# Attention scores from split halves of q and k in float32r, and maxima with a separate mask pass

## The chip, the cores and the metric

The kernel runs on one core of a Trainium2 chip. The metric is the device time of one execution in microseconds. A core has five engines that run their own instruction streams: TensorE (PE; its weight loads are shown apart as PEld), VectorE (DVE), ScalarE (ACT), GpSimd (POOL) and SyncE (SP), which here only issues DMAs. Engines wait for one another through semaphores. SBUF is the working memory of 128 partitions; TensorE writes to PSUM, which has eight banks of 128 partitions by 512 float32 numbers.

## The reference, cut to what matters

One transformer block for 8 batches of 1024 tokens of width 256, with 16 heads of 16 dimensions each. `ca`, `sa`, `ga`, `cb`, `sb` and `gb` are rows computed from a small conditioning input.

```python
h = _layernorm(x, axis=-1) * (1 + ca) + sa
qkv = jnp.einsum('bnd,ed->bne', h, w_in)
...
scores = jnp.einsum('bhqd,bhkd->bhqk', q, k) * Hd ** (-0.5)
scores = jnp.where(causal, -jnp.inf, scores)
attn = jax.nn.softmax(scores, axis=-1)
out = jnp.einsum('bhqk,bhkd->bhqd', attn, v)
...
x = x + ga * (out @ w_out.T + b_out)
h = _layernorm(x, axis=-1) * (1 + cb) + sb
xr = mu_r * h + (1.0 - mu_r) * h_prev      # h_prev: h one token earlier
xk = mu_k * h + (1.0 - mu_k) * h_prev
x = x + gb * (sigmoid(xr @ W_r.T) * (square(relu(xk @ W_k.T)) @ W_v.T))
```

The change concerns the causal scores, their maxima over the keys, and the exponentials of score minus maximum.

## The kernel before, in words

**Units, steps and strips.** Attention is worked in units of four heads: `u` counts 32 units, four to a batch. Four heads lie on the 128 partitions in strips of 32 (`ST`): 16 partitions with the head's q or k, the rest padding. A matmul over one strip uses 32 rows of TensorE, so four heads can run beside one another. A unit has nine steps (`STEPS`, `ORDER`): a to e are the blocks on the causal diagonal, 0 to 3 the whole blocks below it. Each step covers about 512 score columns for each of the four heads. A pass over a unit is made twice.

- In the pass **S** (`maxima`, line 513) the queries stand on the partitions of the result: tile `pp` (two heads of one half, two PSUM banks, from a pool of two such tiles). VectorE takes maxima over the keys. On the diagonal this is one custom instruction per head and part, which adds the mask and reduces, with an accumulator read behind it (`largest`, 548); below the diagonal one reduction over two heads.
- `subtract` (577) turns the maxima of 512 queries by a TensorE transpose (`pmx`), negates them on ScalarE (`mrow`) and sends them by one DMA into a padding row of the unit's q tile, where k has ones. So the maximum is subtracted by the product itself.
- In the pass **T** (`weights`, 604) the keys stand on the partitions of the result: tiles `pw`, one bank each from a pool of four that nearly all other products share. ScalarE takes the exponentials, GpSimd zeroes the blocks' upper triangle. `attend` (652) multiplies with v into `po`, some steps at a time (`GROUPS`).

The pass T follows S by `LAG` = 9 steps (line 54), that is by one unit. `step` (1060) records one step: the DMAs that have come due (`transfers`, 155; urgent ones first), the products of both passes, the reductions and exponentials, and then a list of other work placed by hand in the tables `POST`, `PREP` and `END` (1150 to 1186): the projections and layer norms of the next batch, the feed-forward part of the batch before. S takes its steps in the order a, 0, b, e, c, d, 1, 2, 3, T in the order of `ORDER`.

**Order on the engines.** The wrapper `InOrder` (115) keeps each engine's instructions in the order in which they are recorded. All of them therefore have line 125 in the profile, and the reader goes by tile names. All DMAs but three go through SP's queue, where a transfer that waits holds all that follow.

**q and k.** `qk` (448) projects 128 columns of q or k for 512 tokens, ScalarE scales or copies them (`qk`, three buffers), and one DMA writes them into padded scratch in DRAM. `to_chip` (502) loads q and k of a unit back, in strips, into one of `KEPT` = 4 pairs of tiles, by two DMAs. For units 0 and 1 `direct` (489) computes them in place from weights that are padded already.

**Scores.** In `maxima` and `weights` each block is one float32 matmul per head:

```python
pe.matmul(
    pw[n2][:, cols],
    kk[rs, kt * P : (kt + 1) * P],
    q[rs, c * CW + lo : (c + 1) * CW],
    start=True,
    stop=True,
)
```

With both passes under way, first the products of T for heads 0 and 1 are issued beside those of S for heads 2 and 3, then the other way round, part by part.

Of the kernel before, what the change touches and what calls it, by code (L numbers as in the profile page):

```python
# [8 lines left out]
F32 = mybir.dt.float32  # L9
AF = mybir.ActivationFunctionType  # L10
# [19 lines left out]
KEPT = 4  # L30
# [42 lines left out]
def adaln_block(  # L73
# [94 lines left out]
    def load_xa(b, c):  # L168

        place = dict(tag="xb", bufs=3) if (b, c) == (0, 1) else dict(tag="xa")  # L170
        A[b, c]["xa"] = sb.tile([P, NT, D], F32, name=f"xa{b}_{c}", **place)
        sync.dma_start(A[b, c]["xa"], tokens(x, b, c))
# [40 lines left out]
    wgate = const.tile([P, DC, 2, D], F32, tag="wgate", name="wgate")  # L213
# [22 lines left out]
    q_of, k_of = [], []  # L236
    for u in range(KEPT):
        q_of.append(const.tile([P, N], F32, tag=f"q{u}", name=f"q{u}"))
        k_of.append(const.tile([P, N], F32, tag=f"k{u}", name=f"k{u}"))

    zero = const.tile([P, 1], F32, tag="zero", name="zero")
    one = const.tile([P, 1], F32, tag="one", name="one")
    pool.memset(zero, 0.0)
    pool.memset(one, 1.0)

    def clear_strips(u):
        act.copy(q_of[u], zero.to_broadcast([P, N]))
        act.copy(k_of[u], one.to_broadcast([P, N]))
# [4 lines left out]
    for n in range(2 * NC):  # L253
# [3 lines left out]
    padded_of = [  # L257
        [
            [
                dram.tile([NC, 2 * HG, ST, CW], F32, tag=f"pad{m}{n}{half}", name=f"pad{m}{n}{half}")  # L260
                for half in range(2)
            ]
            for n in range(2)
        ]
        for m in range(2)
    ]

    def clear_dram(m, half):
        for n, of in enumerate((q_of[3], k_of[3])):
            for c in range(NC):  # L270
                sync.dma_start(padded_of[m][n][half][c, :, HD:, :], of[:, :CW])
# [7 lines left out]

    def row_of(t):  # L280

        return strips(t)[:, HD, :]
# [57 lines left out]
    def fold(b, n):  # L340
        gate = G[b]["gates"]
        name, of = (("wo", wo_sb), ("wv", wfv_sb))[n]
        G[b][name] = sb.tile([P, DC, D], F32, tag=f"{name}b", bufs=2, name=f"{name}b{b}")
        for c in range(DC):
            pool.tensor_mul(G[b][name][:, c, :], of[:, c, :], gate[:, n * D : (n + 1) * D])
        if n == 0:
            G[b]["bias"] = sb.tile([P, D], F32, tag="biasb", bufs=2, name=f"biasb{b}")
            pool.tensor_mul(G[b]["bias"], b_bc, gate[:, :D])
# [79 lines left out]
    def prep(b, c):  # L428
# [19 lines left out]
        def qk(n, half):  # L448
# [7 lines left out]
            w = sb.tile([P, CW], F32, tag="qk", bufs=3, name=f"qk{b}_{c}_{n}_{half}")  # L456
            if n == 0:
                act.mul(w, pq, SCALE)
            else:
                act.copy(w, pq)  # L460

            later(lambda: sync.dma_start(padded_of[b % 2][n][half][c, :, :HD, :], w))
# [25 lines left out]

    def direct(c, n, g):

        pq = bank(f"pd{c}_{n}_{g}")
        for d in range(DC):
            of = padded[d][:, n * H + g * HG : n * H + (g + 1) * HG, :].rearrange("p h e -> p (h e)")
            by_strips(pq, of, A[0, c]["hT"][:, d, :], d == 0, d == DC - 1)
        to = (q_of, k_of)[n][g][:, c * CW : (c + 1) * CW]
        if n == 0:
            act.mul(to, pq, SCALE)
        else:

            act.activation(to, pq, AF.Identity, bias=below)  # L500

    def to_chip(u):

        b, g = divmod(u, NG)
        for n, of in enumerate((q_of, k_of)):
            heads = slice(g % 2 * HG, (g % 2 + 1) * HG)
            sync.dma_start(
                of[u % KEPT].rearrange("p (c n) -> p c n", c=NC),
                padded_of[b % 2][n][g // 2][:, heads].rearrange("c h s n -> (h s) c n"),
            )  # L510


    def maxima(u, k, half):
# [3 lines left out]
        q, kk = q_of[u % KEPT], k_of[u % KEPT]  # L517
        js = (2 * half, 2 * half + 1)
        pp = ps_s.tile([P, 2, CW], F32, tag="s", name=f"pp{u}_{k}_{half}")
        parts, at = [], 0  # L520
        for c, i, diagonal in STEPS[k]:
            if ("max", c) not in V:

                V["max", c] = sb.tile(
                    [P, c + 1, HG * NT], F32, tag=f"max{c}", bufs=2, name=f"max{u}_{c}"
                )
            t = NT - 1 - i if diagonal else i
            n = (t + 1) * P if diagonal else CW
            parts.append((c, t, slice(at, at + n), diagonal))
            at += n  # L530

        def products(m):
            if m >= len(parts):
                return
            c, t, cols, diagonal = parts[m]
            q0 = c * CW + t * P
            k0 = c * CW if diagonal else 0
            for n2, j in enumerate(js):
                rs = slice(j * ST, (j + 1) * ST)
                pe.matmul(  # L540
                    pp[:, n2, cols],
                    q[rs, q0 : q0 + P],
                    kk[rs, k0 : k0 + cols.stop - cols.start],
                    start=True,
                    stop=True,
                )

        def largest():
            for c, t, cols, diagonal in parts:
                n = cols.stop - cols.start  # L550
                mx = V["max", c][:, 0 if diagonal else 1]
                to = mx.rearrange("p (j t) -> p j t", t=NT)[:, js[0] : js[0] + 2, t]
                if diagonal:

                    for n2 in range(2):
                        dve.tensor_tensor_reduce(
                            out=pp[:, n2, cols],
                            in0=pp[:, n2, cols],
                            in1=mask[:, CW - n :],
                            scale=1.0,  # L560
                            scalar=-3e38,
                            op0=ALU.add,
                            op1=ALU.max,
                            accum_out=to[:, n2 : n2 + 1],
                        )
                else:
                    dve.tensor_reduce(to, pp[:, :, cols], AX.X, ALU.max)

        return products, largest

    def join(u, c):
        V = U[u]
        if c:
            mx = V["max", c]
            dve.tensor_max(mx[:, 0], mx[:, 0], mx[:, 1])

    def subtract(u, c):

        V = U[u]
        mx = V["max", c]  # L580
        pt = bank(f"pmx{u}_{c}")

        pe.transpose(pt[: HG * NT, :P], mx[:, 0], ident)
        row = sb.tile([HG * NT, P], F32, tag="mrow", name=f"mrow{u}_{c}")
        act.mul(row, pt[: HG * NT, :P], -1.0)
        to = row_of(q_of[u % KEPT])[:, c * CW : (c + 1) * CW]
        later(
            lambda: sync.dma_start(
                to.rearrange("j (t n) -> j t n", t=NT),
                row,  # L590
            ),
            urgent=True,
        )

# [9 lines left out]
    def weights(u, k, half):  # L604
# [3 lines left out]
        q, kk = q_of[u % KEPT], k_of[u % KEPT]  # L608
        js = (2 * half, 2 * half + 1)
        pw = [ps_t.tile([P, CW], F32, tag="t", name=f"pw{u}_{k}_{j}") for j in js]  # L610
        parts, total = parts_of(k)

        def products(m):
            if m >= len(parts):
                return
            c, kt, lo, cols = parts[m]
            for n2, j in enumerate(js):
                rs = slice(j * ST, (j + 1) * ST)
                pe.matmul(
                    pw[n2][:, cols],  # L620
                    kk[rs, kt * P : (kt + 1) * P],
                    q[rs, c * CW + lo : (c + 1) * CW],
# [738 lines left out]
```

## Time and profile before

| what | value |
|---|---|
| median of 3 runs (lowest to highest) | 1365.71 us (1365.66 to 1366.23) |
| profiled execution, first to last instruction (its own time; no other is given) | span 1367.6 us |
| granted TensorE clock | 0.996 |
| TensorE: busy, records | 1356.5 us (99%), 14415 |
| VectorE | 1065.4 us (78%), 2879 |
| ScalarE | 873.6 us (64%), 1690 |
| GpSimd | 548.4 us (40%), 841 |
| DMA | 118.55 MB, 26.5% of the 16 DMA engines' time |

The profile is of one execution. Busy time is the union of an engine's instructions; a TensorE record's end is modelled, so records that follow one another overlap in the listing, and start times are the safer thing to read. A line of a group names the engine, the operation, output and inputs by tile name, their shapes and the number of instances; then busy time and mean duration in ns of one; then the engine's idle time just ahead of them and which engine ended it. A stretch gives for each engine its busy time and, in brackets, its number of instructions.

### The profile page before, as it was taken

The numbers are of one execution on the slowest core, as the hardware profiler recorded it, in microseconds if no ns is written. First come the engines' busy times: TensorE is split into PE (matmuls) and PEld (weight loads), VectorE is DVE, ScalarE is ACT, GpSimd is POOL, SyncE is SP. The second block draws the span as 40 slices with busy tenths as digits, with TensorE's granted clock in tenths as the row PEclk, the third lists the DMA queues.
The fourth block names the chain that finished last, engine by engine and source line by source line (L and its number), as shares of the span: only waits on it lengthen the run. The fifth ranks groups of instructions, "written<-read, shape, count | busy, mean of one in ns | idle before, by whom it ended". The sixth has DMA issues, their size and how long they took to land.

```text
span 1367.6 us, 36111 instructions
## 1 busy us (share of the span) xinstructions
PE 1356.5 (99%) x14415; PEld 681.7 (50%) x14415; DVE 1065.4 (78%) x2879; ACT 873.6 (64%) x1690; POOL 548.4 (40%) x841
## 2 busy tenths in 40 slices
PE   9999999999999999999999999999999999999998
PEld 5444445454454544545545544545444455454546
DVE  6787687789878888787877887778888787887735
ACT  3476666666667666766667666676666666566452
POOL 1041243435423464324544354244542344355342
PEclk9999999999999999999999999999999999999999
DMA  6422423132132323223232322423222232211101
GB/s 197 155 68 78 141 76 120 52 106 94 54 118 71 104 87 100 67 72 110 88 117 69 104 68 76 128 64 109 82 90 60 80 110 72 88 45 41 48 20 35
DMA packets 81624, 118.55 MB, mean 87 GB/s; under 512 B 10152, under 2 KB 39720, under 8 KB 81456
## 3 DMA queue, kind: packets, MB, share of 16 engines
q1 hardware_dynamic: 81248, 116.05, 26.5%
q8 instruction: 113, 1.85, 0.6%
q14 instruction: 55, 0.45, 0.1%
q10 hardware_dynamic: 208, 0.20, 0.1%
HBM read 70.63 MB, written 44.55 MB: 84 GB/s over the span
## 4 chain that ended last, share of the span: by engine, by line
PE 95%; DVE 3%; issue 0%; POOL 0%; ACT 0%; DMA 0%; DVEq 0%; POOLq 0%; ACTq 0%
PE pw L125 12%; PE po L125 8%; PE pq L125 8%; PE pp L125 6%; PE po_e L125 5%; PE po_c L125 5%; PE pr L125 4%; PE py L125 4%; PE pv L125 4%; PE pk L125 4%; PE pkv L125 4%; PE pw_a L125 4%; PE pw_c L125 3%; PE pw_e L125 3%; PE pw_b L125 2%; PE pw_d L125 2%
## 5 line engine op out<-in xcount | busy, mean ns | idle before, releaser
L125 DVE TENSOR_REDUCE max<-pp 128x2 f32<-128x1024 f32 x256 | 301.7, 1220 | 53.4 <-PE pp L125 52.6
L125 ACT ACTIVATE w<-pw 128x512 f32<-128x512 f32 x512 | 265.4, 604 | 75.5 <-PE pp L125 51.8
L125 PE MATMUL pw<-q,k 32*128 32x512 f32 x1024 | 262.4, 616 | 0.0
L125 PE MATMUL pp<-k,q 32*128 32x512 f32 x1024 | 257.9, 624 | 0.1
L125 PEld LDWEIGHTS pw<-q,k 32*128 32x128 f32 x1024 | 105.5, 184 | 100.9 <-issue 38.3
L125 DVE DVE_READ_ACCUMULATOR2_ANT max<- 128x1 f32 x1024 | 144.8, 141 | 0.0
L125 DVE CUSTOM_DVE_ANT_0 pp_c<-pp_c,mask 128x256 f32<-128x256 f32 x240 | 102.3, 436 | 41.6 <-PE pp_c L125 35.5
L125 DVE CUSTOM_DVE_ANT_0 pp_e<-pp_e,mask 128x512 f32<-128x512 f32 x128 | 87.9, 707 | 56.0 <-PE pp_e L125 53.8
L125 DVE CUSTOM_DVE_ANT_0 pp_b<-pp_b,mask 128x128 f32<-128x128 f32 x240 | 102.3, 437 | 35.9 <-PE pp_b L125 29.5
L125 DVE CUSTOM_DVE_ANT_0 pp_d<-pp_d,mask 128x128 f32<-128x128 f32 x240 | 102.5, 437 | 28.9 <-PE pp_d L125 22.8
L125 PE MATMUL po<-w,v 128*32 128x512 f32 x1024 | 123.0, 598 | 0.0
L125 PE MATMUL pq<-hT,wqk_sb 128*32 128x512 f32 (+1 forms) x816 | 112.1, 596 | 0.0
L125 POOL TENSOR_TENSOR xb<-xb,r 128x512 f32<-128x512 f32 x30 | 41.8, 1395 | 136.5 <-DVE r L125 111.0
L125 DVE CUSTOM_DVE_ANT_0 pp_a<-pp_a,mask 128x512 f32<-128x512 f32 x128 | 87.8, 707 | 9.3 <-PE pp_a L125 6.6
L125 POOL TENSOR_TENSOR o<-o,more 128x512 f32<-128x512 f32 x62 | 79.1, 1276 | 37.6 <-ACT more L125 37.4
L125 ACT ACTIVATE w_a<-pw_a 128x512 f32<-128x512 f32 x128 | 66.3, 603 | 39.5 <-PE pp_a L125 36.5
L125 POOL TENSOR_TENSOR rsb<-rsb,m_half 128x2 f32<-128x2 f32 x30 | 21.4, 714 | 174.4 <-DVE rsb L125 174.4
L125 PEld LDWEIGHTS pp<-k,q 32*128 32x128 f32 x1024 | 78.8, 183 | 4.5 <-DVE max L125 4.4
L125 ACT ACTIVATE w_d<-pw_d 128x512 f32<-128x512 f32 x120 | 62.3, 602 | 22.9 <-PE pp_e L125 20.6
L125 ACT ACTIVATE w_e<-pw_e 128x512 f32<-128x512 f32 x128 | 66.2, 604 | 14.6 <-PE pp_c L125 13.6
L125 ACT ACTIVATE w_b<-pw_b 128x512 f32<-128x512 f32 x120 | 62.1, 603 | 14.2 <-PE pp L125 13.8
L125 ACT ACTIVATE w_c<-pw_c 128x512 f32<-128x512 f32 x120 | 62.5, 603 | 13.3 <-PE pp_b L125 8.8
(214 smaller groups left out, 2918.1 us busy)
## 6 DMA issues: line engine op xcount, KB each, us to landing
pad<-qk SPq DMA_DIRECT2D x60, 256.0 KB
q<-pad SPq DMA_DIRECT2D x30, 512.0 KB
k<-pad SPq DMA_DIRECT2D x30, 512.0 KB
od<-o SPq DMA_DIRECT2D x60, 256.0 KB
xa<-in_x SPq DMA_DIRECT2D x16, 512.0 KB
xb<-in_x SPq DMA_DIRECT2D x16, 512.0 KB
oT<-od SPq DMA_DIRECT2D x60, 128.0 KB
ov<-over SPq DMA_DIRECT2D x30, 256.0 KB
```

What stands on the lines that cost most here:

```text
L125: made = f(*args, **kwargs)
```

## The change

**Scores.** q and k are each split into an upper half (rounded to float32r) and a lower one (the remainder, also float32r). A strip of k now has its 16 dimensions with upper and lower half on neighbouring partitions, 32 rows. A strip of q exists twice, once with the upper half and once with the lower half of each dimension on both neighbours. The product of k with either q tile gives two of the four half products. S issues two float32r matmuls per block, accumulated in PSUM. T issues three: the third multiplies two rows of ones with the two halves of the negated maximum, which lie in a tile `m` of their own.

**Maxima.** On the diagonal the mask, now 128 columns wide, is added to the diagonal blocks of both heads by one VectorE instruction in PSUM, and the maxima over both heads are taken by one reduction (equal parts: for both parts at once) or one per part.

**Splitting.** After ScalarE's copy of each piece of q or k, GpSimd makes the upper half by a copy and the lower half by a subtraction; two DMAs write them. `to_chip` has three DMAs, two of them reading each row twice. The negated maxima are split by ScalarE and VectorE and sent by two DMAs. `direct` uses weights with each column doubled and splits on ScalarE and VectorE.

**Order.** The two halves of a step become two streams (T of heads 0 and 1, then S of the same; S of heads 2 and 3, then T), from which matmuls are taken so that the columns issued stay even.

**Room.** `KEPT` goes from 4 to 3 (of three tiles each), the x tiles of the second part from three buffers to two, the folded output weights and bias from two to one, the pieces `qk` from three buffers to four; q and k of a unit are loaded one unit later, x of the second part later (`-7 x.load; -3 x.bias` for `-12` and `-6`), and the end's table is moved accordingly. The clearing of the padding in DRAM goes.

In instructions: TensorE from 7385 in the program to 11988, VectorE from 2881 to 1690, ScalarE 1695 to 1698, GpSimd 846 to 965, DMAs through SP 507 to 645.

```diff
-KEPT = 4
+KEPT = 3
...
-            w = sb.tile([P, CW], F32, tag="qk", bufs=3, name=f"qk{b}_{c}_{n}_{half}")
+            w, hi = (
+                sb.tile([P, CW], F32, tag="qk", bufs=4, name=f"qk{b}_{c}_{n}_{half}{h}")
+                for h in range(2)
+            )
...
-            later(lambda: sync.dma_start(padded_of[b % 2][n][half][c, :, :HD, :], w))
+            hi, lo = hi.bitcast(F32R), w.bitcast(F32R)
+            pool.tensor_copy(hi, w)
+            pool.tensor_sub(lo, w, hi.bitcast(F32))
+
+            def away():
+                to = (q_in, k_in)[n][b % 2][half]
+                for h, of in enumerate((hi, lo)):
+                    sync.dma_start(to[:, h, c * CW : (c + 1) * CW], of.bitcast(F32))
...
+        sync.dma_start(
+            k_of[u % KEPT].bitcast(F32), k_in[b % 2][g // 2][of].rearrange("d s n -> (d s) n")
+        )
+        for h in range(2):
             sync.dma_start(
...
+                qs_of[u % KEPT][h].bitcast(F32),
+                q_in[b % 2][g // 2][of, h, :].unsqueeze(1).to_broadcast([HG * HD, 2, N]),
             )
...
+            for h in range(2):
+
+                def products(h=h, q0=q0, k0=k0, n=n, at=at):
+                    for n2, j in enumerate(js):
+                        rs = slice(j * ST, (j + 1) * ST)
+                        pe.matmul(
+                            pp[:, n2, at : at + n],
+                            qs[h][rs, q0 : q0 + P],
+                            kk[rs, k0 : k0 + n],
+                            start=h == 0,
+                            stop=h == 1,
+                        )
...
+            by = mask.unsqueeze(1).unsqueeze(1).to_broadcast([P, 2, len(parts), P])
+            dve.tensor_add(on, on, by)
+            if equal:
+                dve.tensor_reduce(of[:, :, 0:2, t], both, AX.X, ALU.max)
+                return
+            begin = 0
+            for c, t, n, _ in parts:
+                dve.tensor_reduce(of[:, :, c, t], pp[:, :, begin : begin + n], AX.X, ALU.max)
+                begin += n
...
+        act.mul(hi, of, -1.0)
+        dve.scalar_tensor_tensor(lo, of, -1.0, hi.bitcast(F32), ALU.mult, ALU.subtract)
+        V["m", c] = sb.tile([P, CW], F32R, tag="m", bufs=3, name=f"m{u}_{c}")
...
+            for h in range(3):
+
+                def products(c=c, kt=kt, lo=lo, cols=cols, h=h):
+                    for n2, j in enumerate(js):
+                        at = j * ST
+                        if h < 2:
+                            rs = slice(at, at + ST)
+                            left = kk[rs, kt * P : (kt + 1) * P]
+                            right = qs[h][rs, c * CW + lo : (c + 1) * CW]
+                        else:
+                            left = ones[at : at + 2, :]
+                            right = V["m", c][at : at + 2, lo:]
+                        pe.matmul(pw[n2][:, cols], left, right, start=h == 0, stop=h == 2)
...
+        took = [0, 0]
+        while any(lists):
+            s = min((s for s in range(2) if lists[s]), key=lambda s: (took[s], s))
+            cols, products, after = lists[s].pop(0)
+            took[s] += cols
+            products()
+            if after:
                 after()
```

## The prediction

> **What bounds the kernel now.** I read the page first (busy shares, the chain that ended last), then busy time by stretch, then TensorE's timeline of one batch, then the groups of VectorE. The page:
>
> ```profile
> span 1367.6 us, 36111 instructions
> PE 1356.5 (99%) x14415; PEld 681.7 (50%) x14415; DVE 1065.4 (78%) x2879; ACT 873.6 (64%) x1690; POOL 548.4 (40%) x841
> PE 95%; DVE 3%; issue 0%; POOL 0%; ACT 0%; DMA 0%; DVEq 0%; POOLq 0%; ACTq 0%
> ```
>
> TensorE is never without work and carries 95% of the chain. That it is 99% busy does not say that it streams at its peak, so I look at what its time is made of. Busy time by stretch (microseconds, PE, PEld, DVE, ACT, POOL, clock, DMA share, GB/s), first the prologue, then one batch of the steady middle, then the end:
>
> ```profile
> 0.00:52.20 52.20, 48.92 (x385) 23.35 (x385) 35.95 (x107) 18.47 (x26) 6.46 (x23) 1.00 0.55 179
> ...
> 408.60:569.40 160.80, 160.71 (x1792) 80.50 (x1788) 130.66 (x354) 108.22 (x210) 68.57 (x104) 1.00 0.28 89
> ...
> 1206.40:1367.60 161.20, 155.74 (x1428) 84.78 (x1424) 101.72 (x246) 85.86 (x171) 69.79 (x103) 0.99 0.12 35
> ```
>
> One batch is four units (four heads each) of nine steps, 36 steps in 160.8 us, or 40.2 us a unit. The second busiest engine, VectorE, has 30.1 us left in a batch; 26 of these are waits for TensorE's products, the rest short gaps, so VectorE is occupied for about 134.9. That is the next floor, only 16% below.
>
> TensorE's timeline of two steps (start, duration, operation, count):
>
> ```profile
> 416.54 0.48 PE L125 MATMUL pw_c<-q,k 32*128 32x256 f32 x2
> 416.55 0.49 PE L125 MATMUL pp_b<-k,q 32*128 32x128 f32 x4
> 416.86 0.38 PE L125 MATMUL pw_c<-q,k 32*128 32x256 f32 x2
> ...
> 418.65 1.09 PE L125 MATMUL ptb<-ident,hb 128*128 128x128 f32 x8
> 419.58 3.60 PE L125 MATMUL pq<-hT,wqk_sb 128*128 128x512 f32 x8
> ...
> 437.40 0.70 PE L125 MATMUL pw<-q,k 32*128 32x512 f32 x2
> ...
> 439.37 0.42 PE L125 MATMUL py<-wob,oT 128*32 128x256 f32 x4
> ```
>
> The scores of step c last from 416.54 to 418.65 (2.11 us), those of step 0 from 437.40 to 439.37 (1.97). Adding the nine such bursts of one unit gives 17.9 us, so 71.4 of a batch's 160.8 are scores; the other 89.4 are not changed. In the program a float32 matmul is one instruction; here it has two records (step 0 issues 8 and has 16). The 8 records of pq on the whole array take 3.60 us, 0.45 for 512 columns each. In step 0 16 such records take 1.97, 0.123 each: the four strips of 32 rows do run beside one another.
>
> **The change on TensorE.** It puts two float32r matmuls in place of one float32 one for the maxima, three for the weights (the third adds the maximum). No row shows float32r. Its bounds: a float32r matmul of 512 columns costs at most one whole record of 512 columns (0.123 us in a burst), and at least half of that stream, which is what a float32 record of 256 columns has. Step c prices that: 32 records of 256 columns on average in 2.11 us, **66 ns each**; within a burst equal strips follow at 0.21 us, 53 ns with four side by side. I take 66, since it includes the filling and turning of a burst. For narrower ones (128 to 384 columns) the nearest rows are 128-column records: eight of po_c stand from 427.08 to 427.44 in the timeline, 45 ns each, and those of pp_b are 60 apart on average; I take 50.
>
> Counting the new order over nine steps: a unit has 120 wide and 120 narrow matmuls (four steps of 20 wide; with T in b and d, 8 wide and 24 narrow; T in c, 40 narrow; T in e and 0, 12 wide and 16 narrow). So 120 x 0.066 + 120 x 0.050 = 13.9 us a unit, 55.7 a batch in place of 71.4: **15.7 us saved, TensorE at 145.1**. Bounds: 120 x 0.053 + 120 x 0.045 = 11.8 (47.0 a batch, TensorE 136.4); with whole records, 120 x 0.123 + 120 x 0.066 (the narrow ones are 256 wide on average, which is step c's price) = 22.7 (90.7 a batch, TensorE 180.1).
>
> [...]
>
> **The change on VectorE.** Groups of this batch:
>
> ```profile
> L125 DVE TENSOR_REDUCE max<-pp 128x2 f32<-128x1024 f32 x32 | 37.7, 1220 | 3.4 <-PE pp L125 3.4
> L125 DVE DVE_READ_ACCUMULATOR2_ANT max<- 128x1 f32 x128 | 18.1, 141 | 0.0
> L125 DVE CUSTOM_DVE_ANT_0 pp_c<-pp_c,mask 128x256 f32<-128x256 f32 x32 | 13.6, 436 | 5.7 <-PE pp_c L125 4.9
> L125 DVE CUSTOM_DVE_ANT_0 pp_e<-pp_e,mask 128x512 f32<-128x512 f32 x16 | 11.0, 707 | 8.1 <-PE pp_e L125 7.8
> L125 DVE CUSTOM_DVE_ANT_0 pp_d<-pp_d,mask 128x384 f32<-128x384 f32 x16 | 9.1, 566 | 0.5
> ```
>
> Masked maxima now: one custom instruction and one accumulator read per head and part, from start to start 0.79, 0.66, 0.53 and 0.39 us for 512, 384, 256 and 128 columns; 32 of each a batch make 75.8. After: mask added to 256 or 512 elements (same operands as the custom rows, 0.436 and 0.707) and maxima over two heads (1.220 for 1024; by 1.04 ns an element 0.953 for 768, 0.420 for 256). Steps a and e: 16 halves of 1.656 = 26.5; b and d: 16 of 2.08 = 33.3; c: 8 of 1.927 = 15.4; together 75.2, and 0.04 behind each of the 96 instructions, which now wait one for another: 79.0. The masked part saves instructions and no time. The low half of the row of maxima adds 8 x 0.3 (128 elements: 0.307). So **VectorE goes from 134.9 to 140.5**, and up to 0.5 more at each of the 8 if it has to wait for the transposed maxima: 144.5. At the low end the mask add is cheaper than a custom row, at most by 5.
>
> **Sum.** TensorE 145.1 and VectorE 140.5 to 144.5 a batch, with two score tiles between them, so neither can run ahead by more than about a step. VectorE's heavy steps stand together (S in b, e, c, d: 15 us a unit of maxima against 9.4 in the four steps that only reduce), so there it is the limit and elsewhere TensorE. I add 5 us for that: **150 in place of 160.8**. The steady part (52.2 to 1206.4, 1154.2 us) becomes 1154.2 x 150/160.8 = 1076.7. The end has fewer scores side by side and waits more; half the saving, 154. The prologue is a chain: the first k now needs two ScalarE copies and a VectorE instruction (0.6 + 0.6 + 0.7 for 0.69), 53. Together 1283.7 of the profiled execution; its span was 1.9 over the median of the runs, so 1282.
>
> **What I cost at nothing.** ScalarE: same exponentials, 108.2 of 150. GpSimd: two more instructions per piece of q or k, 8 pieces a batch, at 1.04 (its multiply of 128x512): 68.6 + 16.6 = 85 of 150; behind them wait the writes of q and k, whose first reader, the load of the next unit, comes many steps later. If GpSimd falls behind, SyncE's queue stands at those writes, and the row of maxima behind them. DMA: 118.6 MB become about 150, a share of 0.28 becomes 0.36. Loads of q and k come eight steps ahead, some 33 us, for 1.5 MB; without that cover each late load stops TensorE directly. The row of maxima has a longer way: transposition, ScalarE, now VectorE, now two DMAs. In the one place where the trace has a wait for it (0.7 us), 2.6 us passed from issue to use; elsewhere 3.4 passed without a wait. After: 2.6 + 0.3 + 0.4 (one more issue on SP) = 3.3, against 3.4 less 0.2 of shorter scores plus the rounds ahead of the pass that needs it, some 0.8. So about 0.7 us spare; queued behind the waiting pass is all of TensorE.
>
> **Rivals.**
> - *The scores run at the lower bound* (136.4): then VectorE is the bound, 140.5 plus 2.5 of friction, 143: 1154.2 x 143/160.8 = 1026, with 52 + 150 - 2 = 1226. For it: equal strips do follow at 53 ns.
> - *Narrow matmuls and both engines near full cost more*: narrow at 64 ns (+6.7 a batch), the rest as above, 157: 1127 + 54 + 158 - 2 = 1337. For it: the 60 ns of pp_b. Against: the 45 of po_c.
> - *Slower: the row of maxima comes late.* VectorE's instruction for it stands behind the masked maxima of step a (3.2 us). If VectorE is a whole step late, TensorE stands at the third pass of pw_c once in each of 31 units. It decides from (1366 - 1282)/31 = 2.7 us a unit; a step late less the 0.7 spare, and 1.5 for the restart of ScalarE and VectorE behind it, is 4 us: 1282 + 124 = 1406. Against: VectorE had 26 us of waits a batch, and the score tiles let it be late by one step only.
> - *float32r is no faster per record than float32*, so that the change does not do what it says: 180.1 a batch and friction, 183: 1314 + 54 + 166 - 2 = 1532.
>
> **Chances.** Main case 0.48 (1255 to 1310), lower bound 0.18, the dearer case 0.17, late row 0.10, no gain per record 0.05, within 0.2% 0.02. Faster 0.83, same 0.02, slower 0.15; 0.2% is about what a measurement of this kernel can tell from no change. The range leaves out the last two rivals and the far part of the first: 1200 to 1365.
>
> **What would show it.** float32r records of 512 columns in bursts of 20 in about 1.3 us (2.5 would be the last rival). VectorE over 93% in steady stretches, with masked maxima at 75 to 79 us a batch. Waits of pp's weight loads for VectorE's maxima, new, in steps b to d. No waits of pw_c for the DMA of the row; several us each would be the slower rival. If mask additions into the score tile cost far more than the custom rows, or the strips do not overlap in float32r, the prediction is wrong.

## The result and the profile after

The changed kernel takes 1430.12 us (median of four runs, 1426.42 to 1438.93) where the kernel before takes 1365.68: a ratio of **1.0478, 95% interval 1.0445 to 1.0511. It is slower**; 1282 was predicted, with a range of 1200 to 1365. The profiled execution is the longest of the four (span 1437.0), some 9 us over the median.

From the page of the changed kernel: span, busy time of the engines, the granted clock in forty slices, the chain of waits.

```profile
span 1437.0 us, 38719 instructions
PE 1352.4 (94%) x15946; PEld 730.6 (51%) x15946; DVE 1113.5 (77%) x1688; ACT 874.4 (61%) x1693; POOL 666.9 (46%) x960
PEclk8989999999999999999999999989999999999989
PE 58%; DVE 24%; ACT 5%; POOL 5%; DMA 4%; issue 3%; SPq 0%; ACTq 0%; DVEq 0%; POOLq 0%
```

TensorE is busy for as long as before (1352 against 1356 us), and its idle time went from 11 to 85 us. The chain was 95% TensorE; now 42% of it are others. VectorE, the predicted limit of four steps in nine, is no busier in share than before (77%).

Busy time by stretch of the changed kernel (stretch, length, PE, PEld, DVE, ACT, POOL, clock, DMA share, GB/s): up to the first step of T, up to the last unit's, and the end.

```profile
0.00:66.25 66.25, 53.96 (x386) 25.52 (x387) 43.67 (x85) 18.74 (x29) 13.34 (x30) 0.87 0.36 118
66.25:1324.40 1258.15, 1195.64 (x14617) 644.61 (x14613) 1010.58 (x1493) 807.52 (x1568) 613.23 (x873) 0.96 0.32 107
1324.40:1437.00 112.60, 102.80 (x952) 60.48 (x948) 59.24 (x111) 48.12 (x96) 40.32 (x57) 0.95 0.12 37
```

The same three of before are 52.25, 1207.35 and 108.00, at clocks of 1.00, 1.00 and 0.99. So 14.0 us came in the prologue, 50.8 in the units and 4.6 in the end. Taken from one first step of T to the next, an undisturbed unit lasts 40.1 us, as before (40.1 to 40.4). Batches are counted here and in the expectations as in the prediction, whose batch at 408.60 begins with T's unit 9. The first unit of a batch is then T's unit 5, 9, 13 and so on, the later of the two in which the next batch's q and k are projected. The second unit of a batch lasts 41.0 in four of six, **the first one 45.5 to 48.8**: over the six steady batches the first ones make some 39 of the 50.8 us.

So there are two questions: where the predicted saving in the scores went, and where the loss comes from.

**The saving.** TensorE's timeline of one step 3 of the changed kernel (start, duration, operation, instances):

```profile
465.92 0.50 PE L126 MATMUL pw<-q,k 32*128 32x512 f32 x2
465.93 0.50 PE L126 MATMUL pp<-k,q 32*128 32x512 f32 x2
466.26 0.39 PE L126 MATMUL pw<-q,k 32*128 32x512 f32 x2
466.26 0.40 PE L126 MATMUL pp<-k,q 32*128 32x512 f32 x2
466.49 0.39 PE L126 MATMUL pw<-m,ones 2*128 2x512 f32 x1
466.49 0.39 PE L126 MATMUL pw<-q,k 32*128 32x512 f32 x1
466.49 0.40 PE L126 MATMUL pw<-m,ones 2*128 2x512 f32 x1
466.70 0.49 PE L126 MATMUL pw<-q,k 32*128 32x512 f32 x1
...
467.58 0.42 PE L126 MATMUL py<-wob,oT 128*32 128x256 f32 x4
```

A strip's matmuls do follow at 0.23 us (466.26 to 466.49), so float32r streams 512 columns in the time that was hoped for. But the burst lasts 1.66 us, not 1.32. At 466.49 T's second half starts with one head instead of two; the other head's comes at 466.70. The weight loads of the same stretch and ScalarE's copy say why:

```profile
466.26 0.18 PEld L126 LDWEIGHTS pw<-q,k 32*128 32x128 f32 x1
466.69 0.18 PEld L126 LDWEIGHTS pw<-q,k 32*128 32x128 f32 x1 [0.25 <-ACT more L126]
466.70 0.18 PEld L126 LDWEIGHTS pp<-k,q 32*128 32x128 f32 x2
```
```profile
466.06 0.59 ACT L126 COPY more<-po 128x512 f32<-128x512 f32 x1 [0.70 <-PE po L126]
```

The load waits for ScalarE's copy `more`, which empties the PSUM bank that this head is to write and ends at 466.65. T needs all four banks of its pool; the fourth still holds the last product made before the burst. What was recorded behind this load stands too: `pp`'s load comes at 466.70. TensorE counts as busy meanwhile, because the other strips run. The nine bursts of an undisturbed unit sum to 17.7 us with 240 matmuls, against 17.8 before with 192 records: **nothing was saved**. Step b alone rose, from 1.96 to 3.0 (see below); the other eight fell by 1.1 us together, where 3.9 a unit were predicted.

**The loss.** TensorE's waits in the changed kernel (total us, times, longest):

```profile
PE pw_b L126 <- DVE mrow L126: 20.5, 25, 1.3
PE pw_d L126 <- ACT qk L126: 16.4, 6, 3.9
PE pw L126 <- DVE mrow L126: 4.9, 6, 0.8
PE pta L126 <- DVE ha L126: 4.3, 4, 2.8
```

None of these was in the profile before. The first and third: the transposed maxima stand in a bank of the same pool, and VectorE now reads it as well (the lower half of the row). That instruction stands in VectorE's queue behind other work, so the bank comes back late and step b stops, in a burst of 3.01 us in place of 1.96. The second: ScalarE's copy of a piece of q or k waits for a buffer, and pw_d's bank waits behind it. Then the granted clock. Two stretches of the changed kernel, one behind the other:

```profile
426.78:430.19 3.41, 2.81 (x37) 1.71 (x33) 3.31 (x9) 1.90 (x6) 1.30 (x4) 1.00 0.01 2
430.20:433.60 3.40, 3.34 (x17) 0.59 (x16) 1.13 (x1) 2.47 (x6) 3.40 (x6) 0.50 0.30 98
```

In the second the clock is halved, and the sixteen matmuls of pq, from TensorE's timeline here and in the prologue, take 3.55 us in place of 1.92:

```profile
430.29 3.55 PE L126 MATMUL pq<-hT,wqk_sb 128*32 128x512 f32 x16
```
```profile
44.23 1.92 PE L126 MATMUL pq<-hT,wqk_sb 128*32 128x512 f32 x16 [0.51 <-ACT wqk_sb L126]
```

The trace has 121.6 us at half clock in 28 such episodes; before it has 14.1 us in 3. Of the 13 between T's units 4 and 27, nine stand in first units of a batch and four in units 18, 19, 22 and 23, which last 41.7 to 43.6 us; units of 40.1 us have none.

### The profile page after: what moved, and what is told of

Its sections match the earlier page's. It is cut to its first block, busy times and chain, and to the rows that moved or that the text cites. A ratio compares the mean times of both kernels' runs of the same rounds, so it can differ in the third digit from the quotient of the medians.

```text
span 1437.0 us, 38719 instructions
## 1 busy us (share of the span) xinstructions
PE 1352.4 (94%) x15946; PEld 730.6 (51%) x15946; DVE 1113.5 (77%) x1688; ACT 874.4 (61%) x1693; POOL 666.9 (46%) x960
## 4 chain that ended last, share of the span: by engine, by line
PE 58%; DVE 24%; ACT 5%; POOL 5%; DMA 4%; issue 3%; SPq 0%; ACTq 0%; DVEq 0%; POOLq 0%
DVE max L126 12%; PE pw L126 9%; PE po_c L126 5%; PE po_e L126 4%; PE pr L126 4%; PE pk L126 4%; PE py L126 3%; PE pq L126 3%; PE pv L126 3%; PE po L126 3%; PE pkv L126 3%; DMA kin<-qk 3%; PE pw_e L126 3%; PE pw_d L126 2%; PE pw_c L126 2%
## 5 line engine op out<-in xcount | busy, mean ns | idle before, releaser
L126 PE MATMUL pw<-q,k 32*128 32x512 f32 x1024 | 204.5, 444 | 5.7 <-DVE mrow L126 4.9
L126 PE MATMUL pp<-k,q 32*128 32x512 f32 x1024 | 183.0, 438 | 2.1 <-DVE max L126 2.1
L126 PE MATMUL pw<-m,ones 2*128 2x512 f32 x512 | 124.9, 394 | 0.0
L126 ACT ACTIVATE w_a<-pw_a 128x512 f32<-128x512 f32 x128 | 66.2, 602 | 36.5 <-PE pw_a L126 36.4
L126 POOL TENSOR_TENSOR o<-o,more 128x512 f32<-128x512 f32 x62 | 79.5, 1282 | 18.9 <-ACT more L126 18.9
L126 PE MATMUL pw_b<-q,k 32*128 32x128 f32 x480 | 64.1, 333 | 20.9 <-DVE mrow L126 20.5
L126 POOL TENSOR_TENSOR qk<-qk,qk 128x512 fp32r<-128x512 f32 x60 | 78.9, 1314 | 5.0
L126 POOL CAST qk<-qk 128x512 fp32r<-128x512 f32 x60 | 39.5, 658 | 89.1 <-ACT qk L126 84.7
L126 DVE TENSOR_REDUCE max<-pp_e 128x2 f32<-128x1024 f32 x64 | 78.5, 1226 | 2.2
L126 DVE TENSOR_REDUCE max<-pp_a 128x2 f32<-128x1024 f32 x64 | 78.5, 1226 | 2.2
L126 DVE TENSOR_REDUCE max<-pp_b 128x2 f32<-128x768 f32 x120 | 77.5, 687 | 2.0
L126 DVE TENSOR_REDUCE max<-pp_d 128x2 f32<-128x768 f32 x120 | 77.4, 687 | 2.1
```

What stands on the lines that cost most here:

```text
L126: made = f(*args, **kwargs)
```

## The experiments

**Theory A**: a burst ends with the release of T's last bank, not with the array's work; the loss comes from that bank in step b, from the buffers of the pieces, and from a clock that is halved after stretches in which little of the array works. **Rival B**: each float32r matmul has a price of 88 ns (1.77 us by 20), whatever its place. **Rival C**: VectorE's longer masked part is the limit. The records of all kernels were read for the bursts of steps 1 to 3 between 250 and 1100 us (median from the first score matmul to the next other product) and, over the whole span, for the clock:

| kernel | matmuls in the burst | start of T's second half, its two heads, us | burst, us | at half clock: us, episodes |
|---|---|---|---|---|
| before | 16 records | 0.98, 0.98 | 1.95 | 14.1, 3 |
| the change | 20 | 0.59, 0.88 | 1.77 | 121.6, 28 |
| e1_bank | 20 | 0.58, 0.95 | 1.83 | 88.2, 17 |
| e2_bank_spread | 20 | 0.58, 0.97 | 1.85 | 95.1, 22 |
| e3_s_one_pass | 16 | 0.35, 0.88 | 2.08 | 146.0, 35 |
| e4_s_three_passes | 24 | 0.82, 0.88 | 1.78 | 80.2, 16 |
| e5_zero_passes | 28 | 1.07, 1.07 | 1.86 | 58.0, 12 |
| e7_before_one_pass | 8 | 0.35, 0.89 | 1.38 | 83.2, 14 |
| e9_two_passes_second_half | 18 | 0.58, 0.93 | 1.66 | 98.5, 23 |
| e10_two_passes_first_half | 18 | 0.58, 0.88 | 1.78 | 73.8, 18 |
| e11_two_passes | 16 | 0.58, 0.88 | 1.54 | 102.4, 25 |

A median here stands between three steps that differ, and moves with the stretch (e2_bank_spread: 1.77 between 282 and 1200). Step by step the change has the last head of T's second half at 0.95, 0.93 and 0.78 us in steps 1, 2 and 3, and bursts of 1.82, 1.82 and 1.67. Over its 61 bursts, what follows that start takes 0.88 us, in nine of ten within 0.03; in e11_two_passes, with a round less, it takes 0.66. The same matmuls end earlier where that head starts earlier.

### The bank of the transposed maxima

e1_bank: VectorE takes the lower half of the row from a copy in SBUF.

```diff
+        neg = sb.tile([HG * NT, P], F32, tag="mneg", name=f"mneg{u}_{c}")
+        act.mul(neg, of, -1.0)
         act.mul(hi, of, -1.0)
-        dve.scalar_tensor_tensor(lo, of, -1.0, hi.bitcast(F32), ALU.mult, ALU.subtract)
+        dve.tensor_sub(lo, neg, hi.bitcast(F32))
```

> ScalarE copies the negated maxima to SBUF first and VectorE subtracts there, so that the PSUM bank of the transposed maxima is given back by ScalarE and not by VectorE. Theory A (TensorE stands in step b for that bank, and the clock is cut after such waits): the burst of scores with T in b falls from 3.0 us to about 2.0, each unit loses 1 us, and some cuts of the clock go as well: 1370 to 1395 us. Rival C (VectorE is the limit, TensorE only shows its waits): VectorE has the same work, so within 10 us of 1430.

1402.79 us, ratio to before 1.0267 (1.0244 to 1.0291): 27 us of the loss. TensorE's waits in e1_bank begin with

```profile
PE pw_d L126 <- ACT qk L126: 21.2, 6, 4.1
PE pta L126 <- DVE ha L126: 4.3, 4, 2.8
```

The waits for `mrow` are gone, and the burst of step b fell from 3.01 to 2.24 us. So VectorE's hold on that bank was a cause. The bursts of an undisturbed unit now sum to 17.1 to 17.3 us. The time is 8 us above what A gave; C, which gave no change, is out for this part.

### Room for the pieces of q and k

e2_bank_spread: e1_bank, with the projections of the next batch further apart.

```diff
-    2 n.norm0; 2 m.k0; 2 m.v0; 4 n.norm1; 4 m.v2; 4 m.q1; 6 n.turn; 10 m.k1; 11 n.q0; 11 n.k0;
-    13 n.q1; 13 n.k1; 22 n.v0; 31 n.v2
+    2 n.norm0; 2 m.k0; 2 m.v0; 4 n.norm1; 4 m.v2; 4 m.q1; 6 n.turn; 9 m.k1; 11 n.q0; 13 n.k0;
+    15 n.q1; 17 n.k1; 22 n.v0; 31 n.v2
```

> As e1_bank, and the projections of q and k of the second half stand two steps apart in the table (m.k1 at 9, n.q0 11, n.k0 13, n.q1 15, n.k1 17), since their pieces have four buffers for two halves each. Theory A: the first unit of a batch falls from 46 us to 41 or less, since TensorE no longer stands behind ScalarE's copy that waits for a buffer, and the clock is cut less: 25 to 35 us less than e1_bank, 1340 to 1365. Rival C: no difference to e1_bank.

1397.21 us, 1.0227 (1.0209 to 1.0246). The waits now begin with

```profile
PE pp L126 <- DVE max L126: 11.4, 13, 1.1
PE pta L126 <- DVE ha L126: 3.8, 4, 2.3
```

The 21.2 us for ScalarE's `qk` are gone and step d is undisturbed (2.05 us on average), but 11.4 us of a wait for VectorE's maxima came in its place, and the first unit of a batch still lasts some 45 us (42.4 once). The wait was real, and taking it away gave 5.6 us where A expected 25 to 35: a miss. The cuts of the clock stayed, 22 of them.

### Fewer and more passes for the maxima

e3_s_one_pass takes the products of the maxima with q's upper half alone, e4_s_three_passes adds the lower half a second time (both shift the maxima a little, which the softmax cancels).

```diff
-            for h in range(2):
+            for h in range(1):      # e4: range(3), with qs[min(h, 1)]
```

> S multiplies with the upper half of q only (the lower half's products are left out of the maxima): a burst of step 0 to 3 has 16 matmuls in place of 20. Theory A (a burst is as long as it takes the last PSUM bank of T to come free, some 0.88 us after the start, and three rounds from there): 1.6 to 1.75 us as now (median 1.77), the whole time within 15 us of 1430. Rival B (each float32r matmul of 512 columns costs 88 ns, whatever the order): 1.41 us, and about 3 us less per unit, 1330 to 1345 in all.

> S multiplies with the lower half of q twice (its products count double in the maxima): 24 matmuls in place of 20. Theory A: the added round fills the time in which T waits for its bank; bursts of steps 0 to 3 in 1.75 to 1.95 us, the whole 0 to 30 us longer. Rival B: 24 x 88 ns = 2.12 us, 3 us more per unit, 1510 to 1530.

1502.17 us and 1421.55 us, one run each. Less work made it 72 us slower; more work did not make it slower (5 us under the fastest of the change's four runs, where A gave 0 to 30 more than its median). B is refuted twice: 16 matmuls take 2.08 us, 24 take 1.78. For e3 A had been wrong also; the starts in the table say why. With one pass fewer ahead of it, T's second half reaches the head of TensorE's queue at 0.35 us, waits for its bank until 0.88 all the same, and now T's first half, with its third pass still to come, stands behind it. The exponentials come later, the next product waits for them, and the clock is cut 35 times.

### Passes with zeros

e5_zero_passes: e2_bank_spread with two more float32r passes in each block of S, with a stationary tile of zeros.

```diff
-            for h in range(2):
+            for h in range(4):
...
-                            qs[h][rs, q0 : q0 + P],
+                            (qs[h][rs, q0 : q0 + P] if h < 2 else zeros[rs, :]),
```

> The kernel of e2_bank_spread, with two more float32r passes in every block of the scores whose stationary tile is all zeros, so the result is unchanged: steps 0 to 3 issue 28 matmuls a burst in place of 20. Theory A (a burst ends with the release of the last bank of PSUM and with strips out of step, so more passes fit beside it; and the clock is cut after stretches in which little of the array works): bursts of steps 0 to 3 grow by at most 0.15 us, the cuts fall from 22 to 14 or fewer, the first unit of a batch goes from 45 to about 41 us, and the time is 1355 to 1385 us. Rival B (each matmul has a price whatever the order, 88 ns): 8 more matmuls a burst are 0.7 us a step over 32 steps a unit or so, 1600 us or more.

1418.88 us, 1.0382 (1.035 to 1.0415). (A unit has nine steps, not 32; B's sum is 0.7 us by nine by 32 units.) Of the expectation's three parts two held and the sum failed. Bursts of steps 1 to 3 grew by 0.01 us for eight more matmuls, and the cuts fell from 22 to 12. Stretch 282 to 1200, first of e2_bank_spread, then of e5_zero_passes (the clock is the first number behind the busy times):

```profile
282.00:1200.00 918.00, 895.20 (x11269) 487.50 (x11269) 764.11 (x1124) 613.95 (x1222) 469.46 (x663) 0.98 0.34 111
```
```profile
282.00:1200.00 918.00, 905.89 (x13335) 538.07 (x13331) 762.51 (x1119) 617.83 (x1214) 463.38 (x661) 1.00 0.34 112
```

With more in the array, no cut is left between units 4 and 27 (11 in e2_bank_spread), and the first unit of a batch falls from 45 to 43.1 us. What is left there is in part VectorE: in units 5, 9, 13, 17 and 21 score products wait 1.8 us each for its maxima (`pp` 1.0, `pp_d` 0.6, `pp_b` 0.2), in the units between not at all, but for 0.7 to 0.9 in units 4 and 8. So C, out for step b, holds for a part of this unit. But undisturbed units grew from 39.5 to between 40.0 and 40.4, since in the bursts with narrow blocks the passes are not free (step 0's, beside pp_d, from 1.81 to 2.05), and the prologue by 2.2. The time went up by 22 us where A gave a gain.

### The start

e6_start: e5_zero_passes with the layer norm of the second half recorded ahead of the splitting.

```diff
+    for f in ("stats0", "stats1", "norm0", "norm1"):
+        second[f]()
     direct(0, 0, 0), direct(0, 1, 0)
     twice(1)
-    for f in ("stats0", "stats1", "norm0", "norm1"):
-        second[f]()
```

> The kernel of e5_zero_passes, with the statistics and norm of the second half of the first batch issued ahead of the splitting of q and k. If the 12 to 14 us that the start lost come from VectorE's chain, in which the layer norm now stands behind the splitting, the first T step comes at 58 us or earlier in place of 64.9, and the time is 4 to 8 us under e5_zero_passes. If the start is long because its matmuls run at half the clock, the time is within 2 us of e5_zero_passes.

1410.97 us, 1.0317 (1.0286 to 1.0349): 7.9 us less, as much as expected at most, with the first step of T at 63.8 us in place of 67.1, not at 58. VectorE's order is part of the longer start, and the smaller part. TensorE's timeline of the change's prologue shows the rest:

```profile
13.83 5.35 PE L126 MATMUL pd<-hT,doubled 128*128 128x512 f32 x8 [0.43 <-ACT hT L126]
21.23 0.74 PE L126 MATMUL pp_a<-k,q 32*128 32x512 f32 x8 [2.05 <-DVE k L126]
24.74 0.71 PE L126 MATMUL pta<-ident,ha 128*128 128x128 f32 x2 [2.76 <-DVE ha L126]
```

pd takes 5.35 us at a cut clock (3.70 before), k waits for its third instruction, and the transposes for a layer norm that now stands behind the split; the first two are as they were in e6_start.

### One pass in the kernel before, and the new maxima alone

e7_before_one_pass holds q and k of the kernel before as float32r, one matmul a block; it leaves out the products of the lower halves. e12_before_one_pass is the same again, for an interval. e8_before_new_maxima is the kernel before with the mask added over two heads and the maxima in a pass of their own (one addition more than the change has where two parts differ in width).

```diff
-        q_of.append(const.tile([P, N], F32, tag=f"q{u}", name=f"q{u}"))
+        q_of.append(const.tile([P, N], F32R, tag=f"q{u}", name=f"q{u}"))
```
```diff
-                        dve.tensor_tensor_reduce(
-                            out=pp[:, n2, cols],
...
+                        dve.tensor_add(on, on, by.to_broadcast([P, 2, 1, P]))
...
+                dve.tensor_reduce(to, pp[:, :, cols], AX.X, ALU.max)
```

> The kernel before, with q and k as float32r and one matmul a block of scores; the products that the lower halves carry are left out. Theory A: with a third of the array's work gone from the scores, bursts are 1.2 to 1.4 us in place of 1.96, but the stretches with little work multiply and the clock is cut over 30 times: 1300 to 1400 us. Rival B (the saving of a pass shows in full): bursts of 0.5 to 0.75 us and 1150 to 1200 us.

> The kernel of e7_before_one_pass again, for an interval: one float32r matmul for each block of scores in the kernel before, the products of the lower halves left out. 1240 to 1252 us, a ratio of 0.907 to 0.917.

> The kernel before, with the change's way of adding the maxima and the masks alone: the scores stay float32 products. Theory A: VectorE's part costs nothing of itself, the same within 0.3% of before, 1362 to 1370 us. If VectorE's longer masked part were the cause of the loss (rival C), over 1385 us.

e7: 1245.83 us; e12: 1248.41 us, ratio **0.9131 (0.911 to 0.9151)**. Fewer passes can be had in time: 119 us. A had given 1300 to 1400 us, a miss. The floor is there as well. TensorE's timeline of a step 3 in e7_before_one_pass:

```profile
403.99 0.50 PE L126 MATMUL pw<-q,k 32*128 32x512 f32 x2
403.99 0.50 PE L126 MATMUL pp<-k,q 32*128 32x512 f32 x2
404.33 0.92 PE L126 MATMUL pw<-q,k 32*128 32x512 f32 x2
404.76 0.49 PE L126 MATMUL pp<-k,q 32*128 32x512 f32 x2
405.26 0.42 PE L126 MATMUL py<-wob,oT 128*32 128x256 f32 x4
```

Two rounds of matmuls, 0.43 us at 0.21 a round, take 1.27 us here and 1.38 in the median, since the last head of T's second half starts at 404.76, 0.77 us into the burst (0.89 in the median). A burst of **two rounds is no shorter than what I had predicted for five**. B's 0.5 to 0.75 us is out. The cuts number 14, not over 30: A had overrated them here.

e8: 1380.18 us, 1.0091 (1.0076 to 1.0106). Neither A (the same within 0.3%) nor C (over 1385): VectorE's form has a price of its own, 13.6 us. An undisturbed unit is 0.4 us longer, of which 0.33 stand in one place. TensorE's weight loads in step 1 of e8_before_new_maxima:

```profile
482.38 0.18 PEld L125 LDWEIGHTS pw<-q,k 32*128 32x128 f32 x1 [0.24 <-ACT mrow L125]
482.72 0.29 PEld L125 LDWEIGHTS pw<-q,k 32*128 32x128 f32 x3 [0.16 <-ACT o L125]
483.07 0.30 PEld L125 LDWEIGHTS pp<-k,q 32*128 32x128 f32 x4
```
```profile
481.73 1.29 DVE L125 TENSOR_REDUCE max<-pp_d 128x2 f32<-128x256 f32 x2
```

The burst began at 481.83, and the second half of S gets its tile at 483.07, behind VectorE's maxima of `pp_d`, which end at 483.02; such a burst lasts 2.30 us, 1.97 before. The change itself has 6.8 us of waits for the maxima in all, so the 13.6 cannot simply be added to its other losses.

### The third pass, half by half

On e2_bank_spread, T's third pass is left out in the second half of the heads (e9), the first (e10), or both (e11); the maxima are not subtracted there.

```diff
-            for h in range(3):
+            passes = 3 - half      # e10: 2 + half; e11: 2
+            for h in range(passes):
```

> The kernel of e2_bank_spread without the third pass of the weights in the second half of the heads (each step's second pair of strips): the maxima are not subtracted there, which leaves 18 matmuls in a burst of steps 1 to 3 in place of 20. Theory A: that half starts late, because its last bank of PSUM comes free 0.88 us after the burst's start, so its passes are the end of the burst: 1.85 us falls to 1.5 to 1.6, by the 0.21 to 0.33 us of a round. A price for each matmul or for each round of the array alone: 1.85 falls by 2 of 20, to 1.65 to 1.75, and by as much in e10_two_passes_first_half. Time 1340 to 1400 us.

> The kernel of e2_bank_spread without the third pass of the weights in the first half of the heads: the maxima are not subtracted there, 18 matmuls in a burst in place of 20. Theory A: the first half has its banks from the start and is done before the second, so its third pass lies beside the wait for the last bank: the burst stays within 0.1 us of 1.85. A price for each matmul or round: as much shorter as e9_two_passes_second_half. Time within 20 us of 1397.

> The kernel of e2_bank_spread without the third pass of the weights in either half: the maxima are not subtracted at all, 16 matmuls in a burst. Theory A: no shorter than e9_two_passes_second_half by more than 0.1 us, since the last bank still comes at 0.88 us and two rounds follow: 1.45 to 1.6 us. If the array's rounds alone set the burst (4 rounds of 0.21 us and a start of 0.3), 1.15 to 1.2. Stretches with little in the array multiply, so the clock is cut more often than 22 times: 1340 to 1400 us.

1385.42, 1373.19 and 1350.71 us, one run each. The bursts: 1.66, 1.78 and 1.54 us against 1.85. The same two matmuls cost 0.19 us in the half that waits for the bank and 0.07 in the other, so their place decides, not their number. Step by step it is 0.23, 0.16 and 0.02 us in the waiting half against 0.01 to 0.03 in the other: in step 3, where the bank comes soonest (0.78), neither pass alone is the end. But 1.66 lies just above what A gave, and inside the rival's range for that run alone, and e11 is 0.12 us under e9 where A allowed 0.1. e11 is the clearest: four rounds take 1.54 us, where the rounds alone would give 1.15 to 1.2. The bank comes at 0.88 us in e10 and e11 as in the change. The times follow the bursts only in part (e10, with the longer wide bursts, is faster than e9 and 24 us below e2, more than A gave): it has fewer cuts, and its narrow bursts fell too (step d from 2.04 to 1.82).

No kernel that computes all that the change computes came below the kernel before. e7 and e11 did, and each leaves a part out.

## Why the prediction was wrong

**The step that failed is the price of a record, "I take 66, since it includes the filling and turning of a burst".** It made a burst's time proportional to its matmuls. The runs give 1.38 us for 8, 1.54 for 16 (2.08 in e3's order), 1.77 to 1.85 for 20, 1.78 for 24 and 1.86 for 28; 66 ns each would be 0.53, 1.06, 1.32, 1.58 and 1.85. Only at 28 does the price hold, where T's second half starts at 1.07 us, later than the bank. Below that stands a floor: T's last bank at 0.88 us, and one to three rounds behind it. The kernel before, at 1.95, had its T second half due at 0.98, just after the bank, so its matmuls showed no wait, and I took its bursts for pure streaming. Its weight loads did show the waits; the timeline in the prediction has the matmuls alone. In the kernel before, in the burst at 437.40:

```profile
437.94 0.18 PEld L125 LDWEIGHTS pw<-q,k 32*128 32x128 f32 x1 [0.24 <-ACT mrow L125]
438.29 0.18 PEld L125 LDWEIGHTS pw<-q,k 32*128 32x128 f32 x1 [0.16 <-ACT o L125]
```

The last head's load comes 0.89 us into the burst, behind ScalarE's copy `o`, and its matmul at 438.37. (That burst is T's step 1, not step 0, which stands beside `pp_d` and lasts 1.96 us.) In the change none of the 15.7 us a batch came; without the wait in step b, in e1_bank, 2 to 3 of them do. Seven batches of 15.7 make 110 of the 148 us between forecast and result.

**float32r itself was right**: a round at 0.21 to 0.23 us, as the lower bound had it. The rival "no faster per record" is refuted.

**VectorE was priced rightly and placed wrongly.** Its groups in the changed kernel:

```profile
L126 DVE TENSOR_TENSOR pp_d<-pp_d,mask 128x512 f32<-128x512 f32 x60 | 41.5, 691 | 15.9 <-PE pp_d L126 15.9
L126 DVE TENSOR_REDUCE max<-pp_d 128x2 f32<-128x768 f32 x60 | 57.5, 959 | 2.1
L126 DVE TENSOR_TENSOR pp_e<-pp_e,mask 128x256 f32<-128x256 f32 x64 | 27.4, 428 | 76.3 <-PE pp_e L126 72.7
```

Predicted were 707, 953 and 436 ns. But it does not become the limit: 81% busy between 250 and 1100 us, not over 93%, and 6.8 us of waits for its maxima in all, not one in each of steps b to d. T's units 4 to 26 have none of them. Only when other waits are taken away do they come up there, in the first unit of a batch (1.8 us in most of them in e2, as in e5). e8 shows that its form costs 13.6 us even so; the prediction had put the masked part at 79.0 us a batch for 75.8, and 5 us of friction on VectorE's heavy steps.

**The row of maxima**: I named the transposition, ScalarE, VectorE and two DMAs, and weighed only the arrival. It arrives in time: the profile has no wait of `pw_c` for its DMA. What I left out is that a new reader *holds the bank it reads*. The slower rival had TensorE standing behind VectorE's late instruction, which is so, but at the third pass of pw_c and at 4 us; it is at pw_b, for 0.8 us (20.5 by 25), and e1 prices it at 27 us with what it triggers.

**GpSimd and the pieces, "costed at nothing"**: the cover that I named, a late first reader, covers the data. The four buffers are not covered by it: they hold two pieces, each until GpSimd has split it and a DMA has taken it. ScalarE waited for them, and TensorE for ScalarE (16.4 us). Taking that away gave 5.6 us.

**Friction and the ends.** The prologue was put at 53 us and is 66.2: I counted k's longer chain and neither the layer norm behind the split nor the clock. A steady batch was put at 150 and lasts 166.7 to 174.8.

**The clock, which the working took for 1.00 without a word.** 107.5 us more at half clock are at most 54 us of time, if TensorE is the limit throughout. Each cut lasts 3.41 us or a multiple. For each grid cell of 3.41 us I worked out which share of the array's columns was in use: columns of each record, a quarter for a strip of 32 rows, float32 counted twice, by 2.4 columns a ns (512 in 0.213 us). A quarter is also taken for a strip of 32 columns, and a record counts where it starts. In all fourteen traces together 238 cuts follow a cell, and for 235 of them it was filled to 0.46 or less; in the change the median of the uncut is 0.75, and some 16 of its 358 uncut cells are as low. How busy TensorE was says less: the cell ahead of 430.20 is filled to 0.32 and shows 2.81 of 3.41 us busy, and before other cuts it was busy throughout or, in 1119.70 to 1123.10, not at all. Both a wait and fewer passes in the same time empty the array. e5 fits (zeros in the array, no cuts between units 4 and 27). That little use of the array is what cuts the clock is an account that fits these runs, not one they prove: waits go down in e5 too, and some low cells are not followed by a cut.

The Trainium skill, "TensorE: Matmul & The Clock Gate", under "HAM oscillation — how this bites in real kernels", has as its rule no idle gaps of TensorE over some 3.4 us. The length agrees with the 3.41 us episodes here. The condition fits a few cuts, such as the one behind 1119.70 to 1123.10, where TensorE ran nothing; it does not fit the one at 430.20, ahead of which there are 0.60 us of idle time in all. "Perfetto Trace Analysis", under "Optimization Strategy", says that a gap that comes back again and again can mean too little SBUF or PSUM for the next tile. Loads of `pw` wait for `more` 30 times in the changed kernel, 7.6 us in all, and the 0.25 us above is one of them:

```profile
PEld pw L126 <- ACT more L126: 7.6, 30, 0.6
```

**What stays open.** No run gave T a fifth bank, so the floor is shown by what passes cost on either side of it and by steps whose last head starts at different times, not by taking it away. How much of the 64 us is the clock's was not measured by itself. After e2's mending and with the clock whole, in e5, the first unit of a batch is still 3 us longer than the others; 1.8 of them are the waits for VectorE's maxima, the rest wasn't found.

## What to carry to other kernels

Before a stream of matmuls is shortened, look at what its *last* bank or buffer waits for, and set the new due time of each matmul against the release of what it writes: a release just ahead of the old due time leaves no wait on the matmuls, only on their weight loads, and becomes the floor of the new one. A new reader of a shared PSUM bank, or of a small ring of buffers, is priced by when its queue lets it run, not by its own duration. And a TensorE that is 99% busy with strips of a quarter of the array is not a full array; here kernels with emptier stretches had more cuts of the clock, though waits went with them.

## What the runs showed of the hardware

- float32r with 32 rows: 512 columns follow at 0.21 to 0.23 us, four strips side by side (466.26 to 466.49); 0.33 to 0.35 from the first round of a burst to the second (465.92 to 466.26).
- With more passes of a stationary tile of zeros the cuts of the clock fell, from 22 to 12 in e5_zero_passes.
- Rounding to float32r and subtracting the rounded half, 128x512 each, on GpSimd in the changed kernel (mean ns behind the busy time):

```profile
L126 POOL TENSOR_TENSOR qk<-qk,qk 128x512 fp32r<-128x512 f32 x60 | 78.9, 1314 | 5.0
L126 POOL CAST qk<-qk 128x512 fp32r<-128x512 f32 x60 | 39.5, 658 | 89.1 <-ACT qk L126 84.7
```

The cast took 658 ns where 1.04 us was put for either; the subtraction took 1314.
